# Filling TensorE's waits ahead of the first expert with unread products, and charging its work there by 1.06

## The chip, the cores and the metric

The kernel runs on one core of one Trainium2 chip. The metric is device time in microseconds (us) of one execution, from its start to its end on that core; lower is better. A core has five engines with a queue each: TensorE (PE in the profile, with its weight loads as PEld), VectorE (DVE), ScalarE (ACT), GpSimd (POOL) and SyncE (SP), which here issues the DMA transfers. An engine takes its instructions in the order of its queue; engines wait for each other by semaphores.

## What is computed

One decoder layer in float32: a causal self attention with rotary positions, a cross attention to a context of 361 tokens, and a soft mixture of eight experts, each with a residual.

```python
x = x + _L0_attn_ref(_layernorm(x), Wq, Wk, Wv, Wo)                 # 16 heads of 16
x = x + _L0_xattn_ref(_layernorm(x), ctx_1024, ctx_1024, ...)       # 16 heads of 16
x = x + _L0_ffn_ref(x, norm_gamma, slot_norm_gamma, slot_embeds, w1, b1, w2, b2)
...
logits = einsum('bnd,esd->bnes', xn, sn)
dispatch = softmax(logits, axis=1)                                  # over tokens
combine = softmax(logits.reshape(b, n, e * s), axis=-1)             # over all slots
slots = einsum('bnd,bnes->besd', xn, dispatch)
h = gelu(einsum('besd,edh->besh', slots, w1) + b1)
eo = einsum('besh,ehd->besd', h, w2) + b2
out = einsum('bmd,bnm->bnd', eo, combine)
```

There are 32 images of 100 tokens with 256 features, eight experts of 128 slots each, and a hidden size of 1024.

## The kernel before

**Groups and streams.** The 32 images are taken in eight groups of four. A group's expert work is 64 pairs (group, expert) in all: a first layer into `ph` (16 products of 128x512 for each pair), gelu on ACT, a second layer into `pe` (32 products), and a combination into `py`. Attention for the next group is worked on between the experts' products. It is written as Python generators, called streams: `self_attention`, `cross_softmax`, `crossing`, `cross_queries`, `cross_context`, and, for the mixture, `prepare` (logits), `soften` and `route`. For the first group there is no expert work yet to put it between. So the kernel has a part ahead of the first expert, in which TensorE has only attention, the slots' norms and the first routing to do. This part ends with the call that fills `ready` after `routing = Steps(routes(groups[0], 0))`.

**The account.** The order of instructions is not written by hand, and no run-time scheduler makes it: while the program is built, the Python code keeps an account of when each engine would be free. `pe["t"]` is TensorE's time in it. `spend` (called by `matmul` and `transpose`, whose lines 290 and 294 are the lines of nearly all TensorE work in the profile) adds 0.00084 us for each column and pass, times `pe["slow"]`. This factor is 1.25 ahead of the first expert and is set to 1.0 once `prepare(0)` is done. Work of the other engines is given to `job` with a duration written beside it (`vec`, `act`, `gps`), and `run` issues those whose planned start is not past `pe["t"]`.

A stream yields a `Need`: what must have been written and which PSUM banks must be free. `drive` takes a ready stream's next step; where none is ready, `advance` moves TensorE's time to the next event:

```python
    def advance(*times):
        nxt = run()
        ahead = [t for t in (*times, nxt) if t is not None and t > pe["t"]]
        assert ahead, "nothing left that could go on"
        pe["t"] = min(ahead)
```

So a wait of TensorE exists in the account as a step of `pe["t"]` in `advance`, and in the program only as an order and semaphores.

**PSUM.** Scores use two tiles of two banks each, `sc0` and `sc1` (`rings["pairs"]`, shape 128x2x512 float32, shown as sc in the profile). Self scores take columns 0 to 399 of each bank (`HG * S` = 400), cross scores 0 to 360; only the logits' transposes in `prepare` (`ps_l`) take all 1024 columns. DVE zeroes both tiles at the start (line 564). Everything else uses single banks.

**Names in the steps.** xh is a normalised image from POOL (line 698), xhT its transpose; qk the rotary queries and keys before rotation; p the self scores on their way through the softmax; kT and xv keys and values of the context; xpT the transposed cross probabilities; xav and av the attention outputs; o a projection; rn the slots' norms (POOL, line 603), sq their squares (ACT, line 597), se the loaded slots. psWk, psWq, psWv and psWo are transposes of weights. xnmax (line 1162) is the maximum over cross scores, line 1172 their exponential.

Of the kernel before, what the change touches and what calls it, by code (L numbers as in the profile page):

```python
# [23 lines left out]
def decoder_layer(ctx: ExitStack, tc: tile.TileContext, a: dict, out: bass.AP):  # L24
# [8 lines left out]
    nc = tc.nc  # L33
    x, cx = a["x"], a["ctx_1024"]
    B, S, D = x.shape
# [41 lines left out]


    COL, PIPE, HOP, LOAD = 0.00084, 0.25, 0.15, 1.28
    pe = {"t": 0.0, "slow": 1.25}  # L80
    waiting = {e: [] for e in ("DVE", "ACT", "POOL", "SP")}
    idle_from = {"DVE": 0.0, "ACT": 3.0, "POOL": 5.0, "SP": 0.0}
    tables = {"now": None, "gelus": 0}
# [11 lines left out]
    class Buf:  # L95
# [2 lines left out]

        def __init__(self, make=None, prev=None, before=(), ap=None, root=None, psum=False):
            self.make, self.prev, self.before, self.ap, self.root = make, prev, before, ap, root  # L100
            self.psum = psum
            self.writes, self.uses = [], []

        def get(self):
# [86 lines left out]
    def ends(items):  # L191
        t = 0.0
        for i in items:
            e = i if isinstance(i, float) else i.end
            if e is None:
                return None
            t = max(t, e)
        return t
# [64 lines left out]
    def advance(*times):  # L263

        nxt = run()
        ahead = [t for t in (*times, nxt) if t is not None and t > pe["t"]]
        assert ahead, "nothing left that could go on"
        pe["t"] = min(ahead)

    def hold(items, fill=None):  # L270

        while True:
            run()
            t = ends(items)
            if t is not None and (t == 0.0 or t + HOP <= pe["t"]):
                return
            if fill is None or not fill():
                advance(None if t is None else t + HOP)

    def spend(cols, passes, share):  # L280
        pe["t"] += passes * (COL * cols / share + (0.012 if share > 1 else 0.0)) * pe["slow"]
# [88 lines left out]
    def drive(goal, *streams):  # L370


        while goal.it:
            run()
            ready = [s for s in streams if s.fits()]
            if ready:
                min(ready, key=lambda s: s.need.seq).step()
            else:
                advance(*(s.time() for s in streams))
        return goal.result  # L380
# [117 lines left out]
    def load_constants():  # L498

        load_raw(nc.scalar, "Wk", 5.0)  # L500
        load_raw(nc.scalar, "Wq", 6.5)
        nc.scalar.dma_start(out=rope, in_=a["rope"].rearrange("p (m f) n -> p m f n", f=2))
        load_raw(nc.sync, "Wv", 9.0)
        load_cross("Wk", 10.0)
        rows = R["hT"].new("rows")
        for r0, src in (
            (BQ, a["L0_xattn_bq"].rearrange("(c p) -> c p", p=P)),
            (BK, a["L0_xattn_bk"].rearrange("(c p) -> c p", p=P)),
            (0, a["L0_ffn_b1"].rearrange("e (c p) -> (e c) p", p=P)),
            (NGM, a["L0_ffn_norm_gamma"].rearrange("(c p) -> c p", p=P)),  # L510
            (SGM, a["L0_ffn_slot_norm_gamma"].rearrange("(c p) -> c p", p=P)),
        ):
            nc.sync.dma_start(out=rows.get()[r0 : r0 + src.shape[0], :P], in_=src)
        rows.written(13.0)
        load_raw(nc.sync, "Wo", 14.0)
        load_cross("Wv", 15.0)
        nc.sync.dma_start(out=bvB, in_=a["L0_xattn_bv"].partition_broadcast(P))
        nc.sync.dma_start(out=boB, in_=a["L0_xattn_bo"].partition_broadcast(P))
        load_cross("Wq", 17.5)
        load_cross("Wo", 18.5)  # L520
        se = R["w1"].new("se")
        return rows, se
# [938 lines left out]
    def prepare(g):  # L1461

        nb, nt = SIZES[g], SIZES[g] * S
        nm, cs, diag = R["cnm"].new(), R["cs"].new(), R["diag"].new()
        for b0 in range(0, nb, 2):
            m = min(2, nb - b0)
            for i in range(b0, b0 + m):
                yield free(lambda: len(turning) > 0)  # L1470
                k, at = turning.pop(0)
                assert at == i
                yield Need(k.xns[i])
                transposed(
                    k.xns[i], lambda: k.xn.get()[:, i, :],
                    lambda i=i: k.xnT.get()[:, :, i * S : (i + 1) * S], k.xnT,
                )
            yield free(lambda: state["slots"].it is None and state["routed"] >= NE - 1)
            if b0 == 0:
                k.logits()  # L1480
            cols_ = slice(b0 * S, (b0 + m) * S)
            for e in range(0, NE, 2):
                yield Need(k.xnT, snT)
                ps = bank("ps_lt")
                pv = ps.get().rearrange("p (e n) -> p e n", e=2)[:, :, : m * S]
                for i in range(2):
                    for dc in range(ND):
                        matmul(
                            pv[:, i, :], lhsT=snT.ap[:, dc, (e + i) * NS : (e + i + 1) * NS],
                            rhs=k.xnT.get()[:, dc, cols_],  # L1490
                            start=(dc == 0), stop=(dc == ND - 1),
                        )
                lt = k.lt[e // 2]
                act(
                    0.5, lambda lt=lt, pv=pv: nc.scalar.copy(lt.get()[:, :, cols_], pv), [ps], [lt],
                    prio=0,
                )
                vec(
                    0.57,
                    lambda e=e, pv=pv, ps=ps, b0=b0, m=m: nc.vector.tensor_reduce(  # L1500
                        k.mx.get()[:, e : e + 2, b0 : b0 + m],
                        pv.rearrange("m e (b n) -> m e b n", b=m), axis=AX.X, op=ALU.max,
                    ),
                    [ps], [k.mx], prio=0,
                )

            for b in range(b0, b0 + m):
                if g > 0 and b0 + 2 < nb:
                    mine = logit_squares(k, b, nm, cs)
                else:  # L1510
                    yield Need(*k.lt, banks=0, pairs=1, exps=(1.4, 4.0))
                    ps = rings["pairs"].new("ps_l")
                    pv = ps.get().rearrange("n h s -> n (h s)")
                    for e in range(NE):
                        transpose(
                            pv[:S, e * NS : (e + 1) * NS],
                            k.lt[e // 2].get()[:, e % 2, b * S : (b + 1) * S], ident,
                        )
                    warm("exp")
                    mine = nm.part()  # L1520
                    vec(
                        1.2,
                        lambda b=b, pv=pv: nc.vector.tensor_reduce(
                            nm.get()[:, b : b + 1], pv[:S], axis=AX.X, op=ALU.max, negate=True
                        ),
                        [ps], [mine], prio=0,
                    )
                    act(
                        1.28,
                        lambda b=b, pv=pv: nc.scalar.activation(  # L1530
                            pv[:S], pv[:S], AF.Exp, bias=nm.get()[:, b : b + 1],
                            accum_out=cs.get()[:, b : b + 1],
                        ),
                        [ps, mine], [cs.part()], table="exp", prio=0,
                    )
                vec(
                    0.27,
                    lambda b=b: nc.vector.tensor_scalar(
                        diag.get()[:, b, :], ident[:S, :S], nm.get()[:, b : b + 1], None, ALU.mult
                    ),  # L1540
                    [mine], [diag],
                )
        k.ci = R["cinv"].new()
        vec(
            0.18, lambda: nc.vector.reciprocal(k.ci.get()[:, :nb], cs.get()[:, :nb]), [cs], [k.ci]
        )

        yield Need(diag)
        ps = bank("ps_nm")
        matmul(  # L1550
            ps.get()[:, :nt], lhsT=ones, rhs=diag.get()[:, :nb].rearrange("k b n -> k (b n)"),
            start=True, stop=True,
        )
        k.nmB = R["nmB"].new()
        act(
            0.49, lambda: nc.scalar.copy(k.nmB.get()[:, :nt], ps.get()[:, :nt]), [ps], [k.nmB], prio=0
        )
# [222 lines left out]
    pe["t"] = 1.5  # L1780
    run()
    rows, se = load_constants()
    make_constants()
    load_slots(se)
    slots_kept.append(se.kept())
# [12 lines left out]
    def order():  # L1798
        return (*streams[:2], steps, *streams[2:])
# [14 lines left out]

    routing = Steps(routes(groups[0], 0))
    ready = drive(routing, routing, *order())
    w = weights
    todo = [(g, e) for g in range(NG) for e in range(NE)]
    for i, (g, e) in enumerate(todo):
# [115 lines left out]
```

## Time and profile before

| What | Value |
|---|---|
| Median of 3 runs | 2900.55 us (2897.71 to 2901.32) |
| Profiled execution | 2904.49 us, of which the span of instructions is 2902.5 us |
| TensorE busy in the span | 2855.3 us (98%), mean granted clock 0.987 |
| DVE, ACT, POOL busy | 1519.4, 1190.6, 557.3 us |
| First product of an expert (`ph`) | at 241.02 us |

In the page's picture of the span each digit is the busy share of one fortieth of it, about 72.6 us, in tenths, and the row PEclk gives the clock that TensorE was granted in the same way. A table of windows gives busy times for a stretch of the span; a record of the timeline has a start, a length, and the idle time ahead of it with what ended that. A product in float32 shows as two records, a transpose as one.

### The profile page before, as it was taken

What the parts mean: (1) busy time and instruction counts of PE and PEld (TensorE: products, weight loads), DVE (VectorE), ACT (ScalarE), POOL (GpSimd) and SP (SyncE); (2) the same over time, 40 slices, a digit from 0 to 9 for tenths busy, and PEclk for the clock granted to TensorE, in tenths of its full rate; (3) what the DMA queues carried; (4) which work ended last, traced back from release to release, by engine and by line L of the source; (5) the groups of instructions that cost most, each with busy time, mean ns of one, the idle gap of its engine ahead of it and who ended that gap; (6) DMA issues with size and microseconds to landing.
All of it is one profiled execution on the core that took longest, in us unless ns stands there. A gap on an engine that the chain in (4) does not pass through costs nothing.

```text
span 2902.5 us, 42479 instructions
## 1 busy us (share of the span) xinstructions
PE 2855.3 (98%) x16609; PEld 1982.1 (68%) x16609; DVE 1519.4 (52%) x2831; ACT 1190.6 (41%) x2538; POOL 557.3 (19%) x729
## 2 busy tenths in 40 slices
PE   7989999999999999999999999999999999999999
PEld 5765667676667676676667667677666766676676
DVE  5676565565455556456465465555555555423121
ACT  3544444443434434444443444434434434333331
POOL 4331321022210322112220211202221021100000
PEclk8988999999999999999999999999999999999999
DMA  3015564555554554555464464554555455533231
GB/s 109 11 50 181 175 214 147 190 165 173 167 184 152 188 171 155 185 171 178 154 204 158 141 218 148 192 184 139 185 177 175 163 182 171 175 93 100 78 98 53
DMA packets 331542, 446.34 MB, mean 154 GB/s; under 512 B 18280, under 2 KB 300880, under 8 KB 331344
## 3 DMA queue, kind: packets, MB, share of 16 engines
q1 hardware_dynamic: 330656, 442.90, 46.8%
q8 instruction: 132, 2.16, 0.3%
q10 hardware_dynamic: 688, 0.73, 0.1%
q14 instruction: 66, 0.54, 0.1%
HBM read 300.82 MB, written 142.74 MB: 153 GB/s over the span
## 4 chain that ended last, share of the span: by engine, by line
PE 92%; DMA 3%; DVE 3%; ACT 1%; POOL 1%; issue 1%; SPq 0%; ACTq 0%; DVEq 0%; POOLq 0%
PE pe L290 30%; PE ph L290 30%; PE sc L290 5%; PE sl L290 4%; PE py L290 4%; PE ps_lt L290 3%; PE ps_xv L290 3%; PE ps_xav L290 2%; PE ps_kT L290 2%; PE ps_o L290 2%; PE ps_qk L290 2%; PE ps_av L290 1%; PE ps_v L290 1%; PE ps_xq L290 1%; DMA xpT<-xd 1%; PE ps_xpT L294 1%
## 5 line engine op out<-in xcount | busy, mean ns | idle before, releaser
L290 PE MATMUL pe<-w,hT 128*128 128x256 f32 x4096 | 980.4, 383 | 0.0
L290 PE MATMUL ph<-slT,w 128*128 128x512 f32 x2048 | 965.7, 598 | 0.5
L290 PEld LDWEIGHTS pe<-w,hT 128*128 128x128 f32 x4096 | 751.6, 190 | 159.3 <-issue 50.2
L1693 ACT ACTIVATE hT<-ph,cols 128x512 f32<-128x512 f32 x512 | 351.7, 687 | 816.2 <-PE ph L290 816.0
L290 PEld LDWEIGHTS ph<-slT,w 128*128 128x128 f32 x2048 | 372.0, 190 | 314.7 <-issue 285.5
L1172 ACT ACTIVATE sc<-sc,xnmax 128x361 f32<-128x361 f32 x448 | 238.0, 531 | 175.6 <-DVE xnmax L1162 168.2
L1162 DVE TENSOR_REDUCE xnmax<-sc 128x2 f32<-128x722 f32 x256 | 221.5, 899 | 167.9 <-PE sc L290 167.5
L1186 DVE STREAM_TRANSPOSE xt<-sc 128x384 f32<-128x384 f32 x448 | 230.5, 554 | 21.5 <-ACT sc L1172 15.1
L1592 POOL TENSOR_TENSOR dT<-dT,ri 128x400 f32<-128x400 f32 x64 | 54.9, 858 | 964.8 <-DVE ri L1589 964.8
L891 POOL TENSOR_TENSOR p<-p,nmax 100x800 f32<-100x800 f32 x64 | 96.7, 1523 | 421.3 <-DVE nmax L884 404.5
L1747 DVE SCALAR_TENSOR_TENSOR x<-py,cinv,x 100x256 f32<-100x256 f32 x256 | 112.0, 475 | 115.5 <-PE py L290 114.9
L667 POOL TENSOR_SCALAR ve<-bnmv 100x1 f32<-100x1 f32 x96 | 23.2, 244 | 724.3 <-DVE bnmv L664 674.2
L1724 DVE TENSOR_TENSOR eo<-pe,b 128x512 f32<-128x512 f32 x128 | 87.2, 681 | 137.9 <-PE pe L290 137.1
L290 PE MATMUL sc<-kT,xqT 32*128 32x361 f32 x1024 | 130.5, 532 | 9.5 <-ACT p L1172 4.5
L290 PEld LDWEIGHTS sl<-disp,xn 100*128 100x128 f32 x1024 | 134.4, 192 | 7.2 <-ACT sc L1172 0.6
L290 PE MATMUL sl<-disp,xn 100*128 100x128 f32 x1024 | 135.1, 275 | 0.0
L290 PE MATMUL py<-eo,cT 128*100 128x256 f32 x512 | 131.5, 379 | 0.8 <-DVE eo L1724 0.8
L290 PEld LDWEIGHTS py<-eo,cT 128*100 128x100 f32 x512 | 85.5, 167 | 50.0 <-issue 27.2
L874 DVE TENSOR_TENSOR p<-sc,causal 100x800 f32<-100x800 f32 x64 | 60.4, 985 | 106.2 <-PE sc L290 106.1
L811 DVE STREAM_TRANSPOSE st<-p 128x1024 f32<-128x1024 f32 x56 | 113.6, 2029 | 0.1
L1660 DVE TENSOR_SCALAR slT<-sl,cols 128x512 f32<-128x512 f32 x128 | 93.2, 728 | 37.7 <-PE sl L290 37.7
L1241 DVE TENSOR_TENSOR xoT<-ps_xav,rb 128x100 f32<-128x100 f32 x64 | 16.7, 260 | 180.9 <-PE ps_xav L290 180.8
(155 smaller groups left out, 3243.4 us busy)
## 6 DMA issues: line engine op xcount, KB each, us to landing
w<-in_L_ffn_w_dram SPq DMA_DIRECT2D x512, 256.0 KB
xd<-xt SPq DMA_DIRECT2D x112, 768.0 KB
xpT<-xd SPq DMA_DIRECT2D x112, 768.0 KB
sd<-st SPq DMA_DIRECT2D x70, 512.0 KB
pT<-sd SPq DMA_DIRECT2D x70, 512.0 KB
dd<-dt SPq DMA_DIRECT2D x56, 256.0 KB
disp<-dd SPq DMA_DIRECT2D x56, 256.0 KB
ctx<-in_ctx_dram SPq DMA_DIRECT2D x32, 256.0 KB
```

Of the source, the lines that this page charges most:

```text
L290: nc.tensor.matmul(out, lhsT=lhsT, rhs=rhs, **kw)
L811: lambda: nc.vector.transpose(st.get().rearrange("p j h u -> p h j u"), p.get()[:, hs, :].rearrange("p h (u j) -> p h j u", j=4),),
L874: lambda i=i, hs=hs: nc.vector.tensor_tensor(p.get()[:S, hs, :S].rearrange("n (q h) k -> n q h k", q=2), sc[i].get()[:S, :, : HG * S].rear ...
L891: lambda hs=hs: nc.gpsimd.tensor_tensor(p.get()[:S, hs, :S], p.get()[:S, hs, :S], nmax.get()[:, hs].unsqueeze(2).to_broadcast([S, HPC, S]) ...
L1162: lambda nm=nm, sc=sc: nc.vector.tensor_reduce(nm.get(), sc.get()[:, :, :SK], axis=AX.X, op=ALU.max, negate=True),
L1172: nc.scalar.activation(to[:, :SK], sc.get()[:, i, :SK], AF.Exp, bias=nm.get()[:, i : i + 1], accum_out=sums.get()[:, c, q, r : r + 1],)
L1186: nc.vector.transpose(t_.get()[:, :, :, 2 * t + i, :].rearrange("p j c u -> p c j u"), sc.get()[:, i, : NKB * P].rearrange("p (c u j) -> p ...
L1592: lambda: nc.gpsimd.tensor_tensor(dT.get()[:, :nb, :S], dT.get()[:, :nb, :S], ri.get()[:, :nb].unsqueeze(2).to_broadcast([P, nb, S]), ALU. ...
L1660: lambda dc=dc, sl=sl: nc.vector.tensor_scalar(slT.get()[:, dc, : nb * NS], sl.get()[:, : nb * NS], cols.ap[:, NGM + dc : NGM + dc + 1], N ...
L1693: lambda h=h, ph_=ph_, hc=hc: nc.scalar.activation(h.get()[:, :n], ph_.get()[:, :n], AF.Gelu, bias=cols.ap[:, e * NHC + hc : e * NHC + hc ...
L1724: lambda eo=eo, po=po, m=m: nc.vector.tensor_tensor(eo.get()[:, :m], po.get().rearrange("p (i d) -> p i d", i=2)[:, :m], b2.get().unsqueez ...
L1747: lambda b=b, i=i: nc.vector.scalar_tensor_tensor(xs[g].get()[:, b, :], py[:S, i, :], k.ci.get()[:, b : b + 1], xs[g].get()[:, b, :], ALU. ...
```

## The change

First, in the account, TensorE's work ahead of the first expert is charged by 1.06 in place of 1.25. Second, while a list `awake` is not empty (from the loading of the constants to the end of the first routing), every step of `advance` adds its length to `pe["idle"]`, and for every 0.4 us of it one product is put into TensorE's queue: the 128x128 identity, times 112 columns of the identity, into columns 400 to 511 of the second bank of `sc0`. Nobody reads them. Where the newest use of `sc0` is one of the logits (`whole`) and is not over in the account, none is put and the idle time isn't counted.

```diff
-    pe = {"t": 0.0, "slow": 1.25}
+    pe = {"t": 0.0, "idle": 0.0, "slow": 1.06}
...
-            self.psum = psum
+            self.psum, self.whole = psum, False
...
+        keep_awake(min(ahead) - pe["t"])
         pe["t"] = min(ahead)
+
+    def keep_awake(wait):
+        if not awake:
+            return
+        now = rings["pairs"].past[::2][-1:]
+        if now and now[0].whole and (ends(now[0].uses) or 1e9) > pe["t"]:
+            return
+        pe["idle"] += wait
+        while pe["idle"] > 0.4:
+            nc.tensor.matmul(
+                rings["pairs"].tiles[0][:, 1, HG * S :], lhsT=ident, rhs=ident[:, : 512 - HG * S],
+                start=True, stop=True,
+            )
+            pe["idle"] -= 0.4
...
+    awake = []
...
                     ps = rings["pairs"].new("ps_l")
+                    ps.whole = True
...
     rows, se = load_constants()
+    awake.append(True)
     make_constants()
...
     ready = drive(routing, routing, *order())
+    awake.clear()
```

The added products don't advance `pe["t"]` themselves: the account regards them as lying inside the wait. Since planned durations enter the order, the factor changes the order of the other work ahead of the first expert too.

## The prediction

> **What bounds the kernel now.** I read the page first, then the stretches before and after the first expert, then the granted clock in windows of a few microseconds there, then TensorE's timeline and waits of that part, and the chain of waits last.
>
> ```profile
> PE   7989999999999999999999999999999999999999
> DVE  5676565565455556456465465555555555423121
> PEclk8988999999999999999999999999999999999999
> ```
>
> ```profile
> 0.00:241.00 241.00, 204.50 (x1640) 149.93 (x1641) 165.12 (x313) 109.58 (x307) 87.20 (x123) 0.86 0.23 71
> 480.00:2902.00 2422.00, 2414.91 (x13485) 1671.74 (x13483) 1215.38 (x2262) 981.89 (x2021) 410.81 (x531) 1.00 0.49 159
> ```
>
> The first fence is the page's picture of the span, the second the table of windows. Its columns are a window's length, then busy time of PE, PE's weight loads, DVE, ACT and POOL, the granted clock, the DMA share and GB/s. From 480 us on TensorE is busy 2414.9 of 2422.0 us at full clock; nothing is to be had there. Ahead of the first expert (241 us) it is idle for 36.5 us and its clock is 0.86. The change can only act here.
>
> ```profile
> 28.00:44.00 16.00, 11.51 (x48) 8.67 (x48) 9.12 (x21) 7.59 (x24) 8.65 (x8) 0.68 0.07 24
> 52.00:60.00 8.00, 7.05 (x34) 5.48 (x34) 4.66 (x10) 2.33 (x4) 5.34 (x5) 0.57 0.02 5
> 60.00:81.00 21.00, 17.35 (x117) 11.43 (x117) 10.72 (x20) 10.84 (x35) 3.85 (x6) 0.67 0.01 2
> 81.00:141.00 60.00, 56.52 (x578) 43.91 (x576) 46.04 (x92) 33.49 (x93) 24.57 (x33) 1.00 0.05 14
> 141.00:155.00 14.00, 12.87 (x85) 8.60 (x86) 7.00 (x13) 8.02 (x25) 0.00 (x0) 0.65 0.01 1
> 182.00:189.00 7.00, 5.39 (x63) 4.90 (x64) 2.89 (x10) 2.91 (x10) 4.85 (x10) 0.55 0.23 73
> 217.00:237.00 20.00, 17.16 (x76) 9.10 (x76) 15.92 (x33) 9.53 (x29) 3.89 (x4) 0.50 0.53 180
> 244.00:247.00 3.00, 2.79 (x50) 2.30 (x51) 0.11 (x2) 0.27 (x1) 2.71 (x4) 0.52 0.31 90
> ```
>
> So the loss comes in seven stretches near half clock, while TensorE is mostly busy. What that costs is seen in equal groups in the timeline:
>
> ```profile
> 12.26 2.03 PE L290 MATMUL ps_qk<-xhT,wTWq 128*128 128x100 f32 x8 [0.41 <-ACT xhT L686]
> 15.79 1.06 PE L294 MATMUL psWv<-ident,rawWv 128*128 128x128 f32 x4
> 24.70 0.66 PE L294 MATMUL psWo<-ident,rawWo 128*128 128x128 f32 x4
> 27.87 4.29 PE L290 MATMUL ps_kT<-ctxT,xwWk 128*128 128x361 f32 x8 [1.88 <-ACT ctxT L1060]
> 74.89 2.82 PE L294 MATMUL ps_xpT<-ident,p 128*128 128x128 f32 x12
> 96.17 1.53 PE L294 MATMUL ps_xpT<-ident,p 128*128 128x128 f32 x12
> 132.71 1.03 PE L290 MATMUL ps_qk<-xhT,wTWq 128*128 128x100 f32 x8
> 147.45 0.88 PE L290 MATMUL sc<-kT,xqT 32*128 32x361 f32 x4 [1.13 <-ACT p L1172]
> ```
>
> A start, a length, the group, and in brackets the idle time ahead. Twelve xpT records take 2.82 us cold and 1.53 warm. The cold spells begin after small holes: 1.88 us ahead of kT, 1.13 us ahead of sc. They end after 4 to 13 us of work. (The first 18 us read 1.00 in the clock column, but psWv took 1.06 us there against 0.66 for psWo: cold too.)
>
> ```profile
> PE ps_xhT L294 <- POOL xh L698: 7.0, 5, 4.3
> PE psWk L294 <- DMA rawWk<-in_L_attn_Wk_dram: 5.8, 1, 5.8
> PE sc L290 <- ACT p L1172: 4.5, 6, 1.5
> ```
>
> The holes are waits for POOL's normalisation and for softmax, many and short. In the chain of waits PE alternates with DVE, ACT and POOL pieces of 0.4 to 2 us, so a faster PE shortens only its own pieces.
>
> **What the Trainium skill says.** "TensorE: Matmul & The Clock Gate", Part 1 (The HAM clock gate): the default clock is half, activity over a window of about 3.4 us raises it, and an idle window lowers it. The trace agrees on the two levels (bins read 0.50 or 1.00), but here 1.1 to 1.9 us of idle time sufficed to lose it. Part 4 (PE-mode transpose) says that transposes don't count as activity in the same way; the fillers are ordinary products, so they should. No run here shows a product with the identity raising it.
>
> **The change part by part.** (1) *No useful product goes.* In the built order 153 products with the identity are added, all ahead of the first expert; 24 before the first xhT, 18 before the second. The other TensorE products are the same in number, by the start of the second pair (287 us in the timeline before) the same work lies behind in both, and from a few products later their order matches to the end. So the difference is the shift of that point.
>
> (2) *Price of a filler:* 128x112 on 128 rows; the nearest row is ps_qk (four products, eight records): 1.03 us warm, 2.03 cold, or 0.25 and 0.5 us each. 153 x 0.25 = 38 us, against 36.5 us of holes before. The account places one per 0.4 us of its own waits, so a wait that is as long as planned covers a warm filler and leaves 0.15 us open; a cold one overruns it by 0.1.
>
> (3) *Fillers wait themselves.* They write columns 400 to 511 of the second bank of sc0; no score lies there, yet 30 of the 153 carry waits on DVE or ACT, which read sc0. The next product stands behind them in TensorE's queue, and some softmax exponentials gained a wait for TensorE. Such a filler comes after the wait, not in it.
>
> (4) *The front.* The first nine wait for DVE's memset of sc0, which ends at 4.56 + 0.91 = 5.5 us; then 9 x 0.5 = 4.4 us cold put psWk at 9.9 instead of 5.8. With psWk 1.0, two fillers 1.0, psWq 0.7, two fillers 0.5, cT 0.8 and eleven fillers 2.75, the first xhT comes at about 16.6 in place of 11.26. After xhT, two fillers and ACT's copy qk starts at 17.4 and is warm (1.97 for 3.6), and the 8.9 us from its end to that of the first self scores stay: 28.3 instead of 24.7, 3.6 late. DVE's p and nmax, POOL's p (3.0), rn (1.65) and xh (1.34) follow in POOL's order; part of it waited for the squares of ACT before, so the second xhT is some 2.6 us late. ACT's and POOL's reorders here (the second ctxT copies before the squares) are covered by this wait. The qk and transposes up to 43 us, if warm, give back about 1.6. Front: +1.0; bounds -1.5 (all warm) and +4 (nothing given back).
>
> (5) *Cold pieces on the chain after it,* cold minus warm of the same groups: 52 to 60 (qk, sc) 2.4; 60 to 81 (xpT 1.36; sc, o, sc, xpT, v, sc 0.64+1.06+0.69+1.29+0.84+0.47) 6.35; 141 to 155 5.0; 182 to 189 (xav 0.98, xpT 1.63, rb) 2.7; 217 to 237 6.3; 244 to 247 1.5. In 217 to 237 DVE is busy 15.92 of 20 us, so no more than 4.1 can come out. Sum 22.0. Next in line there is DVE.
>
> (6) *Fillers without cover after the front:* of 153, 63 stand ahead of the first image's cross scores; the 90 behind take 22.5 us. Idle time from 60 to 241 us was 18.6 us, and warm products make more of it, but not where the account has put the fillers. Bounds 0 (all in waits) and 22.5 (all before ready work); I take a third, 7.5, since the plan has 0.4 us for each 0.25 but about a fifth come after a wait of their own.
>
> (7) *The account at 1.06:* planned durations of TensorE's work fall by 15%, so that streams are interleaved otherwise (the next image's qk after two pairs of cross scores, not before). SP moves three parts of the first w2 behind a context load (one part still precedes se), and a few softmax round trips by one place; their data is needed after 241 us, so 0, bounds -3 to +3 because no row shows it.
>
> Sum: -22.0 + 1.0 + 7.5 = -13.5 us. The profiled span 2902.5 becomes 2889.0; 2.0 us lie around it (2904.5 for that run), while the median of the runs is 2900.55. From the median: 2887.
>
> **The rivals.**
> A, as above: 2887, own range 2879 to 2894. For it: the cold stretches are long and half of them busy; against: the uncovered third is my choice.
> B, all cover: (6) at 0 and (4) at -1.5, so 22 + 1.5 = 23.5 us: 2877. For: 38 us of fillers against 36.5 us of old holes plus new ones; against: the waits of (3).
> C, moved but not shortened: warm, yet fillers and DVE take it back; (6) at 20: 2900. For: DVE has 165 of 241 us, 24.5 of 27 between 155 and 182; against: the chain between 60 and 81 has both DVE and ACT at half.
> D, slower: the fillers behind their own DVE and ACT waits leave holes of about 1 us (xnmax takes 0.90), the clock drops again, and fillers at 0.5 overrun. Half of the 22 is gained (11), the front costs 4, and 50 of the 90 fall before ready work at 0.35 on average (17.5): +10.5, 2911. It decides once the uncovered filler time passes what the clock gives back, (6) over 21 us with all warm or over 10 with half.
> E, the change doesn't do what it says: products of an identity don't raise the clock. Then 90 x 0.5 = 45 us meet 18.6 us of holes, and the front adds 2.6: half of the excess on the path (13.2) gives +16, 2916.
>
> **How the numbers follow.** A 0.53, B 0.13, C 0.16, D 0.13, E 0.05. The likeliest gives 2887. The range reaches from 2875 (B with 2 us more from (7)) to 2903 (C's end), leaving out D, E and tails. Faster by over 0.2% (5.8 us, about what this measurement can tell from no change): A and B with a little of C, 0.67; within: most of C, 0.15; slower: 0.18.
>
> **What would show it.** Right: mean clock ahead of the first expert near 0.95, no stretch of 10 us at 0.50 between 60 and 240 us, first expert's first product near 228 us, the rest as before; fillers of 0.12 us a record; the first xhT near 16.6. Wrong: first product past 238 at a high clock (C: fillers just ahead of groups whose inputs were long there, or DVE without pauses), cold stretches with fillers in them (D, E), or a tail from 300 us that differs by more than 2 us (then (7) counts).

## The result, and the profile after

The changed kernel is slower: a median of 2934.81 us (2928.08 to 2937.95, four runs) against 2899.13 us (2889.65 to 2901.32, four runs) of the kernel before, a ratio of 1.0126 with a 95% interval of 1.0097 to 1.0156. The forecast was 2887 us. The profiled execution took 2928.08 us, the shortest of its four, while the profiled one of before (2904.49 us) was longer than any of its own four; so the two profiles show only 24 of the 36 us.

The page of the changed kernel, its first line and two rows of the picture of the span:

```profile
span 2926.1 us, 43075 instructions
...
PE   8998999999999999999999999999999999999999
...
PEclk8998999999999999999999999999999999999999
```

Against the picture of before, TensorE's first and third slices are one tenth busier and its fourth one tenth less, and the clock differs in the third slice alone, by one tenth upwards. The picture is too coarse to show more, so the table of windows comes next (columns as before: length, busy time of PE, weight loads, DVE, ACT and POOL, granted clock, DMA share, GB/s):

```profile
0.00:267.20 267.20, 230.30 (x1939) 181.74 (x1940) 166.82 (x316) 109.07 (x303) 87.70 (x125) 0.89 0.21 66
58.00:75.00 17.00, 15.09 (x75) 11.63 (x76) 7.01 (x13) 6.02 (x23) 2.07 (x2) 0.63 0.00 1
480.00:2890.00 2410.00, 2408.55 (x13587) 1667.45 (x13586) 1219.11 (x2276) 983.20 (x2025) 415.03 (x538) 1.00 0.49 161
```

The part ahead of the first expert now lasts 267.2 us in place of 241.0. From there to the end it is 2926.1 - 267.2 = 2658.9 us, against 2902.5 - 241.0 = 2661.5 before. So the whole loss lies ahead of the first expert, where the change acts. TensorE is busy 25.8 us longer there, the clock rose only from 0.86 to 0.89, and the second line shows a stretch of 17 us at 0.63 in which TensorE is busy almost throughout, with fillers in it. DVE and ACT work as long as before (166.8 and 109.1 us), spread over more time.

Where in that part the time is lost, by landmarks of the two timelines:

| First start of | before, us | after, us | shift |
|---|---|---|---|
| first xhT | 11.26 | 14.40 | +3.1 |
| second xhT | 36.47 | 35.75 | -0.7 |
| third xhT | 51.51 | 51.23 | -0.3 |
| the first image's xn transpose | 100.70 | 112.56 | +11.9 |
| its logits (lt) | 121.27 | 138.03 | +16.8 |
| second image's logits | 202.83 | 224.08 | +21.3 |
| first expert's first product (ph) | 241.02 | 267.21 | +26.2 |

The timeline after, TensorE alone, at the front and at the end of the part (L281 is the filler, L309 the line of matmuls, L313 that of transposes; a start, a length, the group, the idle time ahead):

```profile
5.63 3.95 PE L281 MATMUL sc<-ident 128*128 128x112 f32 x18 [5.63 <-DVE sc L583]
9.42 0.60 PE L313 MATMUL psWk<-ident,rawWk 128*128 128x128 f32 x4
...
11.78 2.62 PE L281 MATMUL sc<-ident 128*128 128x112 f32 x22
14.40 0.39 PE L313 MATMUL ps_xhT<-ident,xh 100*128 100x100 f32 x2
...
267.21 1.74 PE L309 MATMUL ph<-slT,w 128*128 128x512 f32 x2
```

The nine fillers (18 records) after DVE's memset take 3.95 us, 0.44 us each and so mostly cold; the eleven at 11.78 take 2.62 us, 0.24 each, warm. They delay the first xhT by 3.1 us, and by the second xhT that is gone. Up to 52 us, then, hardly anything is lost against the profile of before. Against the kernel of the same order without fillers (e1_charge_alone below, where the third xhT comes at 49.25 us) it is 2.0 us. Most of the loss comes after that, with the cross attention, and the waits say how. These are TensorE's waits up to 270 us (what waited, for what, us in total, times, the longest):

```profile
PE sc L281 <- DVE xnmax L1181: 8.1, 9, 1.4
PE sc L281 <- ACT p L1191: 6.9, 7, 1.3
PE sc L281 <- DVE sc L583: 5.6, 1, 5.6
...
PE sc L281 <- ACT sc L1191: 2.8, 2, 1.4
PE sc L281 <- DVE p L893: 2.5, 3, 1.1
PE sc L281 <- DVE xt L1205: 2.4, 2, 1.2
```

and these are ACT's, from 50 to 260 us:

```profile
ACT p L1191 <- PE sc L281: 13.0, 7, 4.2
...
ACT sc L1191 <- PE sc L281: 6.7, 2, 5.6
```

The six rows shown are waits of fillers, 28.3 us in all, where the rows left out come to some 9 us. The exponentials of ACT wait 13.0 + 6.7 us for fillers, products that no one reads.

How the two come together is seen at one pair of score tiles. The timeline of all engines in the changed kernel:

```profile
60.14 1.57 PE L309 MATMUL sc<-kT,xqT 32*128 32x361 f32 x4
61.64 0.77 PE L281 MATMUL sc<-ident 128*128 128x112 f32 x2
62.45 0.91 DVE L1181 TENSOR_REDUCE xnmax<-sc 128x2 f32<-128x722 f32 x1 [3.92 <-PE sc L281]
63.41 0.77 PE L281 MATMUL sc<-ident 128*128 128x112 f32 x2 [1.00 <-DVE xnmax L1181]
64.11 1.57 PE L309 MATMUL sc<-kT,xqT 32*128 32x361 f32 x4
64.28 0.56 ACT L1191 ACTIVATE p<-sc,xnmax 128x361 f32<-128x361 f32 x1 [4.16 <-PE sc L281]
...
65.74 0.91 DVE L1181 TENSOR_REDUCE xnmax<-sc 128x2 f32<-128x722 f32 x1 [2.38 <-PE sc L309]
66.74 0.56 ACT L1191 ACTIVATE p<-sc,xnmax 128x361 f32<-128x361 f32 x1 [1.27 <-DVE xnmax L1181]
```

Read it downwards: scores into sc0 (60.14), a filler into the same tile (61.64), the maximum over sc0, which waits for that filler (62.45), a second filler, which waits for the maximum (63.41), and only then the scores into sc1 (64.11), which need neither but stand behind the filler in TensorE's queue. ACT's exponential over sc0 waits for the second filler (64.28). From the first score to the first exponential over sc1 it is 66.74 - 60.14 = 6.60 us. The same pair without fillers (experiment e1_charge_alone, the order of the changed kernel; lines above 281 are 19 lower there):

```profile
56.23 2.58 PE L290 MATMUL sc<-kT,xqT 32*128 32x361 f32 x8
...
57.85 1.92 DVE L1162 TENSOR_REDUCE xnmax<-sc 128x2 f32<-128x722 f32 x2 [0.66 <-PE sc L290]
...
58.85 0.56 ACT L1172 ACTIVATE p<-sc,xnmax 128x361 f32<-128x361 f32 x1 [1.46 <-DVE xnmax L1162]
...
59.94 0.56 ACT L1172 ACTIVATE p<-sc,xnmax 128x361 f32<-128x361 f32 x1
```

Both tiles' scores come in one go (x8), the two maxima follow one another, and the first exponential over sc1 starts 59.94 - 56.23 = 3.71 us after the first score. Two tiles exist so that DVE and ACT read one while TensorE fills the other. A filler between them undoes that, for 2.9 us in this pair, at the same cold clock (0.50 in both).

Only 13 of the 153 fillers stand so, in five pairs; more stand behind both tiles of a pair. Those can hold up the queue too:

```profile
55.90 1.24 POOL L717 TENSOR_SCALAR xh<-x,bnmv,rstd 100x256 f32<-100x256 f32 x1
...
58.24 1.19 PE L281 MATMUL sc<-ident 128*128 128x112 f32 x4 [1.29 <-ACT p L1191]
...
59.22 0.54 PE L313 MATMUL ps_xhT<-ident,xh 100*128 100x100 f32 x2
```

xh is ready at 57.14, but its transpose stands behind fillers that wait for an exponential over sc0, and starts 2.1 us later. Without fillers (e1_charge_alone) the same transpose starts at 55.70, right after xh, ready at 55.64.

### The profile page after: what moved, and what is told of

Its sections match the earlier page's. It is cut to its first block, busy times and chain, and to the rows that moved or that the text cites. A ratio compares the mean times of both kernels' runs of the same rounds, so it can differ in the third digit from the quotient of the medians.

```text
span 2926.1 us, 43075 instructions
## 1 busy us (share of the span) xinstructions
PE 2881.4 (98%) x16915; PEld 2012.1 (69%) x16915; DVE 1519.0 (52%) x2831; ACT 1192.4 (41%) x2539; POOL 558.0 (19%) x729
## 4 chain that ended last, share of the span: by engine, by line
PE 94%; DVE 2%; DMA 2%; ACT 1%; issue 0%; POOL 0%; DVEq 0%; ACTq 0%; POOLq 0%
PE pe L309 30%; PE ph L309 29%; PE sc L309 5%; PE sl L309 4%; PE py L309 4%; PE ps_lt L309 3%; PE ps_xv L309 3%; PE ps_kT L309 3%; PE ps_xav L309 2%; PE ps_qk L309 2%; PE ps_o L309 2%; PE sc L281 1%; PE ps_av L309 1%; PE ps_v L309 1%; PE ps_xq L309 1%; PE ps_xpT L313 1%
## 5 line engine op out<-in xcount | busy, mean ns | idle before, releaser
L309 PE MATMUL pe<-w,hT 128*128 128x256 f32 x4096 | 980.4, 383 | 0.0
L309 PE MATMUL ph<-slT,w 128*128 128x512 f32 x2048 | 966.0, 598 | 0.5
L309 PEld LDWEIGHTS pe<-w,hT 128*128 128x128 f32 x4096 | 750.8, 190 | 160.4 <-issue 50.8
L309 PEld LDWEIGHTS ph<-slT,w 128*128 128x128 f32 x2048 | 371.6, 190 | 315.1 <-issue 285.4
L309 PEld LDWEIGHTS sl<-disp,xn 100*128 100x128 f32 x1024 | 136.1, 194 | 7.6 <-DVE ri L1609 1.0
L309 PE MATMUL sl<-disp,xn 100*128 100x128 f32 x1024 | 137.0, 277 | 0.0
L309 PE MATMUL py<-eo,cT 128*100 128x256 f32 x512 | 131.5, 379 | 0.8 <-DVE eo L1744 0.8
L309 PE MATMUL sc<-kT,xqT 32*128 32x361 f32 x1024 | 128.7, 527 | 0.5 <-ACT sc L1550 0.5
L309 PEld LDWEIGHTS py<-eo,cT 128*100 128x100 f32 x512 | 85.4, 167 | 50.1 <-issue 27.5
```

Source lines behind the costliest of these rows:

```text
L309: nc.tensor.matmul(out, lhsT=lhsT, rhs=rhs, **kw)
```

## The experiments

Each kernel was timed against the kernel before on the same chip. The time of before is 2895.5 us for the first four, 2897.4 us for the next three and 2897.7 us for the last. The fillers don't enter the account, so kernels with the same factor have the same order of all other work. The theories, by the letters that expectations use: O, the order that the factor 1.06 makes costs the time; W, the fillers cost it by waits, their own and those of what waits for them or stands behind them; W2, the narrower form of W, that nearly only those between the cross scores and their softmax do; T, the fillers cost it by keeping TensorE busy ahead of ready work; S, every filler costs alike.

**The factor alone: e1_charge_alone.** The kernel before with one number changed.

```diff
-    pe = {"t": 0.0, "slow": 1.25}
+    pe = {"t": 0.0, "slow": 1.06}
```

> The kernel before with the factor 1.06 alone, no fillers. Theory W (the fillers cost: they wait for the readers of sc0's banks and hold TensorE's queue): the new order of the other work is nearly innocent, 2890 to 2910 us, first ph at 235 to 248 us. Rival O (the new order costs: work interleaved for a faster TensorE than there is): 2920 us or more, first ph past 258.

Measured: 2896.11 us, ratio 0.9992 (0.9979 to 1.0004). The order costs nothing by itself; O falls as the cause alone. First ph came at 233.4 us in this profile. That is 7.6 us ahead of the profile of before, but the medians show no such gain. The profile of before is of a long and cold execution: 2904.49 us at a mean clock of 0.987, where the 31 runs of before timed beside this kernel have medians of 2895.47 us and 0.991. So nothing is built on the 7.6 us. The kernels with the factor 1.06 are compared with this one below.

**The fillers alone: e2_fillers_alone.** The changed kernel in the order of before.

```diff
-    pe = {"t": 0.0, "idle": 0.0, "slow": 1.06}
+    pe = {"t": 0.0, "idle": 0.0, "slow": 1.25}
```

> The changed kernel with the factor left at 1.25: 113 fillers, and all other products in the order of the kernel before. W: slower than before by 10 to 25 us (2910 to 2925), with TensorE idle for some 15 us ahead of fillers. O: at or under the time before, 2885 to 2900.

Measured: 2906.76 us, ratio 1.0033 (1.0020 to 1.0047), with 113 fillers, 19 of them with a wait of their own. The time lies below the 2910 us that W expected at least, and above the 2900 us that O expected at most. The parts cost +0.6 and +11.3 us, the whole 35.7: they act together. TensorE's waits up to 267 us show what the longer planned durations avoided:

```profile
PE sc L281 <- ACT p L1191: 6.3, 6, 1.5
...
PE sc L281 <- DVE xnmax L1181: 0.2, 1, 0.2
```

One filler waits for the maximum here, for 0.2 us, where nine wait 8.1 us in the changed kernel. At 1.06 the account lets TensorE reach a step of `advance` between the two tiles of a pair more often: 13 fillers stand there, in five pairs, and at 1.25 4, in two.

**A filler only where the tile is free: e3_free_tile.** A filler is put into sc0 or sc1, whichever's last use is over in the account, and none if neither is.

```diff
-        now = rings["pairs"].past[::2][-1:]
-        if now and now[0].whole and (ends(now[0].uses) or 1e9) > pe["t"]:
+        for i in range(2):
+            now = rings["pairs"].past[i::2][-1:]
+            t = ends(now[0].uses if now else rings["pairs"].first)
+            if t is not None and t + HOP <= pe["t"]:
+                break
+        else:
             return
...
-                rings["pairs"].tiles[0][:, 1, HG * S :], lhsT=ident, rhs=ident[:, : 512 - HG * S],
+                rings["pairs"].tiles[i][:, 1, HG * S :], lhsT=ident, rhs=ident[:, : 512 - HG * S],
```

> The changed kernel (1.06), but a filler goes only into that score tile, sc0 or sc1, whose readers are over in the account; where neither is free none is put (77 fillers left, 8 with a wait of their own). W: idle time ahead of fillers falls from 28 to under 8 us, and the time falls below that of the charge alone if the clock is worth anything: 2880 to 2895. O: stays with the charge alone, above 2920. A third, T (the fillers' own busy time costs, not their waits): 77 of 153 left, so half the loss, about 2915.

Measured: 2898.09 us, ratio 1.0007 (0.9995 to 1.0018), with 77 fillers of which 8 wait. The loss is gone, as W has it, but the gain that W's 2880 to 2895 hoped for isn't there. T, at about 2915, is off, but since half of the fillers went too it needs the denser filling of e7 below.

**One filler for each step: e4_one_per_wait.** At most one filler for a step of `advance`, which leaves all 30 that wait and takes away 43 that stood in a row.

```diff
-        while pe["idle"] > 0.4:
+        if pe["idle"] > 0.4:
...
-            pe["idle"] -= 0.4
+            pe["idle"] %= 0.4
```

> The changed kernel with at most one filler for each step of the account that has come to 0.4 us of wait: 110 of 153 are left, and all 30 waits on DVE and ACT stay. W: the loss stays nearly whole, 2922 to 2935. T: it falls with the fillers' busy time, by 43 x 0.25 = 11 us, to about 2920 or less. O: as W.

Measured: 2923.88 us, ratio 1.0095 (1.0072 to 1.0118), first ph at 264.2 us. 110 fillers of which 30 wait cost 28.4 us; e2's 113 of which 19 wait cost 11.3, in another order. The loss fell by 7.3 us, between W, which has it nearly whole, and T, which takes off 11, and the interval of the ratio reaches into both; so this run alone doesn't decide. Together with e7, where 124 fillers in the same order cost next to nothing, it shows that the number of fillers isn't what counts, and T in its plain form falls.

**None after cross scores: e5_none_after_cross.** The guard of the logits (`whole`) holds for the cross scores too.

```diff
             for t in ts:
                 held[t] = rings["pairs"].new("xsc")
+                held[t].whole = True
```

> The changed kernel, but the rule that keeps fillers off sc0 while it holds logits holds for cross scores too: 98 of 153 fillers left, 11 with a wait of their own. Theory W2 (the loss is made where a filler stands between the two tiles of a pair of cross scores: it waits for the maximum over sc0, sc1's products stand behind it, and the exponential waits for the filler): nearly all of the loss goes, first ph 233 to 242, 2893 to 2906 us. Rival S (each filler costs alike): 55 fillers of 153 fewer give back 12 of 33 us, first ph near 255, about 2918.

Measured: 2899.67 us, ratio 1.0012 (1.0001 to 1.0023), with 98 fillers of which 11 wait. Fillers after self scores stay, and so do their waits in TensorE's row:

```profile
PE sc L281 <- DVE p L893: 2.5, 3, 1.1
...
PE sc L281 <- ACT p L1192: 1.6, 2, 0.9
```

The first is that of fillers on the self scores, word for word as in the changed kernel, and it costs next to nothing; the waits for xnmax are gone, and with them nearly all of the loss.

**Fillers of next to no work: e6_tiny_fillers.** The kernel of e4 with a product of four columns into 32 partitions in place of 112 into 128. Waits and order are those of e4.

```diff
-                rings["pairs"].tiles[0][:, 1, HG * S :], lhsT=ident, rhs=ident[:, : 512 - HG * S],
+                rings["pairs"].tiles[0][:32, 1, 508:], lhsT=ident[:, :32], rhs=ident[:, :4],
```

> As the run with one filler for each wait, with the same 110 places and the same 30 waits, but each filler is a product of 4 columns into 32 partitions, so that nearly no work is left and the clock is not held. W2: the order of waits alone makes the loss: 2912 to 2935. T (work and not waits): as the charge alone, 2892 to 2900.

Measured: 2914.89 us, ratio 1.0066 (1.0042 to 1.0089), first ph at 252.7 us. TensorE's waits up to 267 us:

```profile
PE sc L281 <- DVE xnmax L1181: 8.3, 9, 1.3
PE sc L281 <- ACT p L1191: 6.9, 7, 1.3
```

They are as many and as long as in the changed kernel. So 17.5 us are the price of the waits with products that do next to no work (0.17 us a record in the median, against 0.28 of the full filler in e4), and the other 10.9 us of e4's 28.4 come with the filler's length. The intervals of the two ratios overlap a little; the first ph says the same, 264.2 - 252.7 = 11.5 us. The mean clock ahead of ph is the same in both (0.88 and 0.87), so it doesn't explain the difference. That the length counts fits a filler's place in a chain of scores, filler, maximum, filler, scores; no run shows this share of the loss apart.

**Free tiles, filled more densely: e7_free_tile_dense.** The kernel of e3 with 0.25 us in place of 0.4.

```diff
-        while pe["idle"] > 0.4:
+        while pe["idle"] > 0.25:
...
-            pe["idle"] -= 0.4
+            pe["idle"] -= 0.25
```

> As the run with fillers into a free score tile alone, with one for each 0.25 us of planned wait in place of 0.4: 124 fillers in place of 77, the same 8 waits of their own. W2: their work lies in waits, so 2893 to 2902, with a clock ahead of the first expert above 0.92. T: 47 x 0.25 = 12 us more, 2908 to 2912. If a warm clock is worth its price at all, below 2893.

Measured: 2900.93 us, ratio 1.0008 (0.9999 to 1.0017), with 124 fillers of which 8 wait. This asks whether a warmer clock shows as a gain when few fillers stand where they wait. The windows ahead of the first expert, first of e1_charge_alone, then of e3_free_tile, then of this kernel, all three with the same order of all other work:

```profile
0.00:233.40 233.40, 193.38 (x1633) 145.88 (x1634) 166.37 (x316) 108.35 (x303) 87.44 (x125) 0.88 0.24 75
```

```profile
0.00:233.50 233.50, 204.14 (x1788) 159.32 (x1789) 165.72 (x316) 108.51 (x303) 87.43 (x125) 0.92 0.24 75
```

```profile
0.00:234.30 234.30, 207.51 (x1882) 164.52 (x1883) 166.47 (x316) 108.39 (x303) 87.47 (x125) 0.95 0.24 75
```

The clock goes from 0.88 to 0.92 to 0.95, and the first expert starts at 233.4, 233.5 and 234.3 us. Without its fillers (124 x 0.24 = 30 us, an estimate from the warm ones above) TensorE is busy for about 177.5 us in the last, 16 us less than in the first, and no gain is left of it. Whether the warmer clock is worth nothing here, or the fillers' own places cost what it gives, these runs don't separate.

**Only after cross scores: e8_only_after_cross.** The opposite of e5: the account of idle time runs as in the changed kernel, but a filler is put only where sc0 holds cross scores that are not over.

```diff
+        held = now and (ends(now[0].uses) or 1e9) > pe["t"]
+        if held and now[0].whole == "logits":
             return
         pe["idle"] += wait
         while pe["idle"] > 0.4:
-            nc.tensor.matmul(
+            if held and now[0].whole == "cross":
+                nc.tensor.matmul(
...
                 held[t] = rings["pairs"].new("xsc")
+                held[t].whole = "cross"
...
-                    ps.whole = True
+                    ps.whole = "logits"
```

> The counterpart: the changed kernel with its fillers only where sc0 holds cross scores whose readers are not over in the account: 57 of 153 left, 24 of the waits of their own among them. W2: these alone make nearly the whole loss, first ph past 255 us, 2915 to 2932. Rival S (each filler costs alike): 57 of 153, about 12 us, near 2909, first ph near 245.

Measured: 2929.04 us, ratio 1.0114 (1.0083 to 1.0146). These are 57 of the 153 fillers, 24 of which wait. TensorE's waits up to 267 us:

```profile
PE sc L283 <- DVE xnmax L1184: 7.9, 9, 1.2
PE sc L283 <- ACT p L1194: 6.9, 7, 1.3
```

They make 31.3 us of the loss, 0.55 us each, over twice the 0.24 us that one takes. The other 96 account for what is left of 35.7, some 4 us, which is in keeping with e5's 2.3. S falls, W2 stands. Of the 57, 13 stand between the two tiles of a pair and 44 behind both; how the 31.3 us divide between these isn't shown. Nor is it a colder TensorE that lengthens the part: its mean clock is 0.89 in the changed kernel, against 0.88 in e1 without fillers.

| Kernel | Fillers, of which wait | Ratio to before | First ph, us |
|---|---|---|---|
| changed kernel | 153, 30 | 1.0126 | 267.2 |
| e8_only_after_cross | 57, 24 | 1.0114 | 262.5 |
| e4_one_per_wait | 110, 30 | 1.0095 | 264.2 |
| e6_tiny_fillers | 110, 30 | 1.0066 | 252.7 |
| e2_fillers_alone | 113, 19 | 1.0033 | 240.6 |
| e5_none_after_cross | 98, 11 | 1.0012 | 236.1 |
| e7_free_tile_dense | 124, 8 | 1.0008 | 234.3 |
| e3_free_tile | 77, 8 | 1.0007 | 233.5 |
| e1_charge_alone | 0, 0 | 0.9992 | 233.4 |

The rows are in the order of the ratio. The time follows the column of those that wait more closely than that of all, if not strictly: e8 has fewer waits than e4 and costs no less. No version beats the kernel before by more than its interval.

## Why the prediction was wrong

It forecast 2887 us and a faster kernel; it is slower by 36 us. By its steps:

**(1), no useful product goes and only the start of the first expert shifts: right.** From there to the end it is 2658.9 us against 2661.5, and between 2660 and 2665 in all eight experiments.

**(2), 0.25 us for a warm filler and 0.5 for a cold one: right.** Measured 0.24 warm, and 0.44 on average for the first nine, which began cold.

**(3), thirty fillers wait themselves: seen, but left without a price.** It said "Such a filler comes after the wait, not in it", and that some exponentials gained a wait. It did not go on to ask what stands behind such a filler on TensorE's queue, and who waits for that: the scores of the other tile, then their maximum and their exponentials. Nor did it say why columns that nobody reads make anyone wait. The Trainium skill, "PSUM — Partial Sum Buffer", section "PSUM bank collisions raise a hardware error", says that two engines must not touch the same bank and group of 32 partitions at once even at different columns, and that guards should go by bank and not by address. The waits of the traces fit that: DVE's maximum reads columns 0 to 360 and still waits for a filler in 400 to 511. No run here shows a collision.

**(4), the front at +1.0 us: a small miss.** The first xhT came at 14.40 us, not 16.6, and the second was 0.7 us early, not 2.6 late. Against e1, which has the changed kernel's order, the fillers made these 3.4 and 1.4 us late, so part of the small sum may be the order's. The nine cold fillers had warmed the clock by 9.42 us, where four records of psWk took 0.60 us and not the 1.0 assumed.

**(5), -22.0 us for warm pieces: failed.** It added cold minus warm durations of groups on the chain as if what comes after each had nothing else to wait for and no filler stood in its place. With 8 waiting fillers in place of 30 and a clock of 0.95 (e7) nothing was gained. Part of the 22.0 us was also read from an unusually cold execution (0.987, as said under e1), so some of the cold spells that were priced aren't in a usual one. Where the gain went can be read, though no run shows it by itself, from the chain of waits, taken in windows of 40 us up to the first ph with the pieces added by engine (each window has a chain of its own, so a sum can exceed the time by a few us):

| us on the chain | e1_charge_alone | e7_free_tile_dense | changed kernel |
|---|---|---|---|
| TensorE, useful | 130.1 | 116.0 | 149.2 |
| TensorE, fillers | 0 | 20.7 | 42.4 |
| DVE | 43.9 | 53.3 | 50.3 |
| ACT and POOL | 40.7 | 35.9 | 18.1 |
| the rest (issue, queues, DMA) | 18.9 | 9.9 | 8.4 |
| sum | 233.7 | 235.8 | 268.4 |

In e7 the useful pieces of TensorE did shrink by 14 us, which is what the step hoped for in kind. Fillers take 21 us on the chain in their stead and DVE 9 us more, while POOL, ACT, DMA and issue take less. Read so, the warm pieces were worth something, and the fillers' time on the chain took it back. In the changed kernel even the useful part grew; that work once beside DVE's and ACT's is now in line with theirs would explain it, but isn't shown. That the clock is worth nothing would say too much: of the 31 runs of before timed beside e5 to e7 the fastest (2891.07 us) has a mean clock of 0.992 and the longest (2905.18 us) 0.987, though whether the clock makes the time there or waits make both stays open.

**(6), +7.5 us for fillers without cover: the step that failed most.** It counted an uncovered filler by its own busy time and bounded that by 22.5 us, the length of the 90 behind the front. Measured, 57 fillers after cross scores cost 31.3 us, more than the bound for all. Of e4's 28.4 us, 17.5 are there even with products of four columns. The bound left out that a filler on a tile in use makes its readers wait for it and its successors wait for the readers.

**(7), the order by 1.06 at 0: right alone** (0.9992, 0.9979 to 1.0004). With the fillers it isn't neutral: it decides where they fall and how many there are, and that is the difference between +11.3 us (e2) and +35.7.

Of the rivals D had the mechanism, fillers behind waits on DVE and ACT, and its sign; its 2911 us was too low since it too priced only fillers that "fall before ready work" and the clock. Its cold holes exist (the stretch from 58 to 75 us at 0.63), but the pair shown above lost 2.9 us against a pair that was just as cold. E is refuted: in the same order the clock rose from 0.88 to 0.95 with fillers. Of the prediction's own signs for being wrong, the profile showed a first product past 238 us, though at 0.89 and so without C's high clock, and "cold stretches with fillers in them (D, E)".

Open: whether a bank that nothing else uses would bring a gain. It wasn't tried; e3 and e7 come close to it and bring none, though 8 of their fillers still wait.

## What to carry to other kernels

An instruction that does nothing useful isn't free because its engine is idle in the plan: it takes a place in an ordered queue and a claim on a buffer, so price what stands behind it and who reads that buffer, and not its length alone. Put such work, if at all, into a bank whose readers are over, never between two buffers that alternate. And before warming a clock, set the time that the fillers take on the chain against what the warm pieces give: in e7 it was 20.7 us against 14, and the first expert came no sooner.

## What had not been expected of the hardware

- A product of four columns into 32 partitions still shows 0.17 us a record (median in e6), against 0.28 us for 112 columns into 128 (e4); made this small, a filler saves over a third of its latency and none of its 30 waits.
- Ordinary products with the identity do raise the clock: 0.88, 0.92 and 0.95 for 0, 77 and 124 fillers in one order. The Trainium skill, "TensorE: Matmul & The Clock Gate", Part 4 (PE-mode transpose), says of products in transpose mode that they don't count as busy in the same way; the fillers aren't in that mode, and no run here tests one that is.
- Being busy isn't enough to be warm: from 58 to 75 us TensorE was busy 15.09 of 17.00 us in the changed kernel, with pauses of 0.7 to 1.3 us ahead of waiting fillers, and was granted 0.63. The pauses needn't be the reason: in e1, without fillers, TensorE was busy for all 8 us from 56 to 64 us and was granted 0.50.
